# Fetching the chosen tokens' rows with indirect DMAs instead of one-hot products

## The chip, the core and the metric

The kernel runs on one core of a Trainium2 chip. The core has five engines, each with a queue of its own: TensorE for matrix products (PE; its weight loads are shown apart, as PEld), VectorE (DVE), ScalarE (ACT), GpSimd (POOL), and SyncE (SP), which here only issues transfers. The engines wait for each other through semaphores, and 16 DMA engines move data between the main memory (DRAM) and the on-chip memory (SBUF). Products land in a third memory, PSUM, from which VectorE or ScalarE must copy them ("evict" them).

The metric is the device time of one execution, in microseconds (us).

## The reference, cut to what matters

The program is a Fourier-layer network on 64 images of 256 x 256, whose output rows are joined with 77 text tokens and sent through one attention layer and one feed-forward layer that processes only a chosen part of the tokens. The change lies in that last layer:

```python
def _L0_ffn_ref(x, attention_mask, wr, br, w1, b1, w2, b2):
    weights = (jnp.einsum('bsd,do->bso', x, wr) + br)[..., 0]
    k = max(1, int(CAPACITY * s))
    kk = k - 1 if k > 1 else 1
    _, idx = jax.lax.top_k(weights, k)
    sel_idx = idx[:, :kk]
    sel = jnp.take_along_axis(x, sel_idx[:, :, None], axis=1)
    h = jax.nn.gelu(jnp.einsum('bkd,dh->bkh', sel, w1) + b1)
    y = jnp.einsum('bkh,hd->bkd', h, w2) + b2
    w_sel = jnp.take_along_axis(weights, sel_idx, axis=1)
    y = y * w_sel[..., None]
    processed = jnp.zeros_like(x).at[batch_idx, sel_idx].set(y)
    return processed + x
```

Each of the 64 samples has 333 tokens of 256 numbers. A router gives every token a weight, the 165 tokens of greatest weight go through the two products with a GELU between them, and their results are put back at the tokens' places, times the weight. All other tokens get zero there. Everything is float32.

## The kernel before

Most of the span is the Fourier network; it is the same in both kernels and plays no part here. The code of the change is the last stage, which works through the samples one by one. It is written for a framework that takes the instructions in the order of the program, looks at their dependencies, gives out buffers from pools, and then orders the instructions of each engine by a cost model of its own. So an engine's queue is not the order of the source: work of neighbouring samples is interleaved. Once built, the order is fixed, and each engine takes its instructions strictly in that order (on TensorE this holds for the products).

The main loop keeps three samples in flight. For sample b it runs:

- `image_rows(b + 2)`: loads the last layer's image in eight pieces `ch` of 1 MB on SyncE's queue (L894) and sums over channels with 32 products (L896, into `hp`); before it come small steps on `am` (L878, L882 on VectorE), the product L884, the eviction `y1`, and the products L889. ScalarE evicts `hp` to `h` (L901).
- `attention(b + 1)`: a layer norm (L910 to L918), transposes of it (L928), products for queries, scores and values (L974, L986, L1000), softmax, transposes of the probabilities (L1015, evicted to `probT`), the products with the values (L1024), then the residual: GpSimd adds a bias to `h` (L1020) and VectorE makes `h1` from it (L1027). A second layer norm gives `z` (the tile is called `fz`).
- `feed_forward(b)`: described below.
- `select(done[1])` for sample b + 1: the router. VectorE computes the weights (L940), three products with a matrix of ones (L945) spread them over all partitions, L947 adds the router's bias, and for each of the three tiles of tokens (128, 128 and 77) VectorE counts how many tokens have a greater weight (L954 to L963). That count is the token's rank, `gt`. L965 turns it into a row of a one-hot matrix: `place[token, rank]` is 1 where the token has that rank. `fw` is the weight where the rank is below 165 and zero elsewhere.

In `feed_forward` the one-hot matrix does the fetching and the putting back, with products on TensorE: `z` times `place` gives the 165 chosen rows, transposed, as `zs` (L1042); `place` is transposed to `back` (L1053); and after the two layers of the feed-forward (L1059, GELU, L1070) and a transpose of their result to `ys` (L1080), `back` times `ys` puts the results at their tokens (L1089), where VectorE multiplies by `fw` and adds `h1 + z` (L1092). GpSimd issues the 17 transfers of the output (L1097, L1101).

Evictions go through the helper `evict`, whose counter `flip` gives every second one of this stage to ScalarE and the others to VectorE. GpSimd's transfers use eight semaphores in turn, so one of them waits until the one eight before it has landed.

Of the kernel before, what the change touches and what calls it, by code (L numbers as in the profile page):

```python
# [8 lines left out]

F32 = mybir.dt.float32  # L10
AF = mybir.ActivationFunctionType
ALU = mybir.AluOpType
AX = mybir.AxisListType
# [3 lines left out]
S = 256  # L17
# [5 lines left out]
TOK = S + TXT  # L23
HID = 1024
EPS = 1e-5
KEPT = max(1, int(0.5 * TOK)) - 1
# [8 lines left out]
def _tables():  # L35

    y = np.arange(S)
    ky = np.arange(M)
    kx = np.concatenate([np.arange(M), np.arange(-M, 0)])
    th = 2 * np.pi * np.outer(y, ky) / S  # L40
    tx = 2 * np.pi * np.outer(y, kx) / S
    grid = np.linspace(0.0, 1.0, S, dtype=np.float32)
    p = np.arange(128)
    out = {}

    def halves(a):
        return a.reshape(2, 128, -1).transpose(1, 0, 2)

    def ravel(*dims):

        return np.unravel_index(np.arange(np.prod(dims)), dims)


    fy = np.zeros((S, 32))
    fy[:, :M], fy[:, M:KX] = np.cos(th), -np.sin(th)
    out["fyt"] = np.tile(fy.reshape(8, 32, 32).transpose(1, 0, 2), (4, 1, 1))
    ex = np.zeros((128, S))
    ex[:KX], ex[KX:2 * KX] = np.cos(tx).T, np.sin(tx).T
    ex[2 * KX], ex[2 * KX + 1] = 1, grid
    for n in range(4):  # L60
        ex[2 * KX + 2 + n, 64 * n:64 * n + 64] = 1
    ex[64:] = ex[:64]
    h, i, hq, r, j = ravel(2, 4, 4, 2, 4)
    hc = 4 * h + hq
    out["exE"] = ex[:, 64 * j + 16 * i + 2 * hc + r]
    out["exO"] = ex[:, 64 * i + 16 * j + 2 * hc + r]
    cs = np.concatenate([np.cos(tx), -np.sin(tx)], 1)
    sc = np.concatenate([np.sin(tx), np.cos(tx)], 1)
    csc = np.concatenate([cs, sc, cs], 1)
    j, b2, hh, g, r = ravel(4, 2, 2, 4, 2)  # L70
    for n in "EO":
        rows = []
        for h in range(2):
            a, b = (2 * h + b2, g) if n == "E" else (g, 2 * h + b2)
            rows.append(csc[64 * a + 16 * b + 2 * (2 * j + hh) + r])
        out["fx" + n] = np.stack(rows, 1)
    ck = np.where(ky == 0, 1.0, 2.0) / (S * S)
    t32 = np.zeros((32, S))
    t32[:M], t32[M:KX] = (np.cos(th) * ck).T, -(np.sin(th) * ck).T
    out["t4"] = np.tile(t32, (4, 1))  # L80
    out["ident"] = np.eye(128)
    out["ones"] = np.ones((128, 128))
    out["chan"] = p[:, None] % C == np.arange(C)[None, :]

    cr = np.zeros((2, 64, 4, 32))
    cr[:, 48, 0, 0] = cr[:, 48, 1, 28] = cr[:, 49, 2, 0] = 1
    for n in range(4):
        cr[:, 50 + n, 3, 24 + n] = 1
    out["crow"] = cr

    out["fyr"] = halves(fy)
    out["fyi"] = halves(np.concatenate([np.sin(th), np.cos(th), np.zeros((S, 8))], 1))
    out["fxn"] = halves(np.concatenate([cs, grid[:, None], np.zeros((S, 15))], 1))
    out["gyr"] = halves(np.repeat(grid[:, None], 128, 1))
    m6 = np.zeros((128, 3, 2, 4, C))
    for g in range(3):
        for r in range(2):
            for k4 in range(4):
                m6[M * r + 4 * g + k4 + 32 * np.arange(4), g, r, k4] = 1
    out["m6"] = m6  # L100
    out["mk4"] = p[:, None] % 4 == np.arange(128)[None, :] // C

    g = grid.astype(np.float64)
    one = np.ones(S)
    gh = np.zeros((128, 3, 2, KX))
    for j, (a, b) in enumerate(((g, one), (one, g), (one, one))):
        m = np.outer(np.exp(-1j * tx).T @ a, np.exp(-1j * th).T @ b)
        for k4 in range(4):
            gh[4 * j + k4] = np.stack([m.real, m.imag])[:, :, k4::4].transpose(2, 0, 1)
    out["gh"] = gh  # L110

    t, g, n, hc = ravel(2, 4, 4, 8)
    x_of = 64 * n + 16 * g + 2 * hc + t
    out["exT"] = ex[:, x_of]
    out["mask4"] = p[:, None] // C == np.arange(4)[None, :]
    tok = np.concatenate([x_of, S + np.arange(TXT)])
    rows = np.stack([x_of[:128], x_of[128:], S + p], 1)
    out["iota"] = np.repeat(np.arange(KEPT)[None, :], 128, 0)
    out["tri"] = tok[None, None, :] < rows[:, :, None]
    out = {k: np.ascontiguousarray(v.reshape(128, -1), np.float32) for k, v in out.items()}  # L120

    mv = np.zeros((4, 32, 16, S), np.float32)
    mv[:, :KX] = t32[None, :KX, None, :]
    mv[:, 28] = grid
    return out, mv.reshape(128, 16 * S)
# [10 lines left out]
def tile_fno_fusion_transformer(ctx: ExitStack, tc: tile.TileContext, a, cst_d, grid_d, out):  # L136
    nc = tc.nc
    x = a["x"].rearrange("b x y o -> b x (y o)")
    B = x.shape[0]
# [3 lines left out]
    small = ctx.enter_context(tc.tile_pool(name="small", bufs=4))  # L143
# [633 lines left out]
    s_, t_ = st  # L777
    tcon = ctx.enter_context(tc.tile_pool(name="tcon", bufs=1))
    inp = ctx.enter_context(tc.tile_pool(name="inp", bufs=7))
    tabt = tables(tcon, "exT", "tri", "cstt")  # L780
    EXT, MASK4, IOTA = tabt("exT"), tabt("mask4"), tabt("iota")
    TRI = tabt("tri").rearrange("p (t j) -> p t j", t=3)
    qrow = tcon.tile([128, C, 1], F32, name="qrow")
    nc.vector.tensor_mul(qrow[:, :, 0], qR, s_)
# [12 lines left out]
    D = S  # L797
# [70 lines left out]
    pb_ = ctx.enter_context(tc.tile_pool(name="tpb", bufs=2, space=PSUM))  # L868
    pp = ctx.enter_context(tc.tile_pool(name="tpp", bufs=6, space=PSUM))

    def psum():
        return pp.tile([128, 512], F32, name="pp")

    def image_rows(b):
        am = ap_.tile([2 * KX, 32 * C], F32, name="am")
# [53 lines left out]
            evict(zT[:, dh, :], ps[:, :TOK], 2)  # L929
        return z, zT  # L930

    def select(z):


        wcol = small.tile([128, 3], F32, name="wcol")
# [10 lines left out]
        wrow = tp.tile([128, TOK], F32, name="wrow")  # L946
        nc.vector.tensor_scalar(wrow, ps[:, :TOK], brB, None, ALU.add)  # L947
        fw = small.tile([128, 3], F32, name="fw")
        place = tp.tile([128, 3, KEPT], F32, name="place")
        for t in range(3):  # L950
            r = rows[t]
# [10 lines left out]
            )  # L962
            nc.vector.tensor_add(gt[:r], gt[:r], eq[:r])  # L963
            nc.vector.tensor_scalar(fw[:r, t:t + 1], gt[:r], float(KEPT), wc[:r], ALU.is_lt, ALU.mult)
            nc.vector.tensor_scalar(place[:r, t, :], IOTA[:r], gt[:r], None, ALU.is_equal)  # L965
        return fw, place

    def attention(h):
        z, zT = layer_norm(h, "a")
        qT = tp.tile([128, 2, TOK], F32, name="qT")  # L970
        for eh in range(2):
# [39 lines left out]
        for jt in range(3):  # L1011
# [2 lines left out]
            for t in range(3):  # L1014
                nc.tensor.transpose(ps[:r, toks[t]], p_[:rows[t], t, toks[jt]], ID[:rows[t], :rows[t]])  # L1015
            evict(pT[:r, jt, :], ps[:r, :TOK], 2)
        h1 = tp.tile([128, 3, D], F32, name="h1")
        for t in range(3):
            r = rows[t]
            nc.gpsimd.tensor_add(h[:r, t, :], h[:r, t, :], boB[:r])  # L1020
# [7 lines left out]
                h1[:r, t, :], ps[:r, :D], sm[:r, t:t + 1], h[:r, t, :], ALU.mult, ALU.add  # L1028
            )
        z = layer_norm(h1, "f")  # L1030
        return h1, z

    kept = [slice(0, (KEPT + 1) // 2), slice((KEPT + 1) // 2, KEPT)]

    def feed_forward(b, h1, z, fw, place):

        zs = tp.tile([128, 2, KEPT], F32, name="zs")
        for dh in range(2):
            ps = psum()
            for t in range(3):  # L1040
                r = rows[t]
                nc.tensor.matmul(  # L1042
                    ps[:, :KEPT], lhsT=z[:r, t, 128 * dh:128 * dh + 128], rhs=place[:r, t, :],
                    start=t == 0, stop=t == 2,
                )
            evict(zs[:, dh, :], ps[:, :KEPT], 2)
        back = tp.tile([128, 2, TOK], F32, name="back")
        for c, k in enumerate(kept):
            n = k.stop - k.start
            ps = psum()  # L1050
            for t in range(3):
                r = rows[t]
                nc.tensor.transpose(ps[:n, toks[t]], place[:r, t, k], ID[:r, :r])  # L1053
            evict(back[:n, c, :], ps[:n, :TOK], 2)
        g = tp.tile([128, HID // 128, KEPT], F32, name="g", bufs=1)
        for hb in range(HID // 128):
            ps = psum()
# [18 lines left out]
        for c, k in enumerate(kept):  # L1076
            n = k.stop - k.start
            ps = psum()
            for dh in range(2):
                nc.tensor.transpose(ps[:n, 128 * dh:128 * dh + 128], yT[:, dh, k], ID)  # L1080
            evict(ys[:n, c, :], ps[:n, :D], 2)
        o = tp.tile([128, 3, D], F32, name="o")
        for t in range(3):
            r = rows[t]
            nc.gpsimd.tensor_add(h1[:r, t, :], h1[:r, t, :], z[:r, t, :])
            ps = psum()
            for c, k in enumerate(kept):
                n = k.stop - k.start
                nc.tensor.matmul(  # L1089
                    ps[:r, :D], lhsT=back[:n, c, toks[t]], rhs=ys[:n, c, :], start=c == 0, stop=c == 1  # L1090
                )
            nc.vector.scalar_tensor_tensor(  # L1092
                o[:r, t, :], ps[:r, :D], fw[:r, t:t + 1], h1[:r, t, :], ALU.mult, ALU.add
            )
        for g in range(4):
            for n in range(4):
# [4 lines left out]
        nc.gpsimd.dma_start(out[b, S:TOK], o[0:TXT, 2, :])  # L1101

    hs = {n: image_rows(n) for n in range(min(2, B))}
    done = attention(hs.pop(0))
    done += select(done[1])
    for b in range(B):
        now = done
        if b + 2 < B:
            hs[b + 2] = image_rows(b + 2)
        if b + 1 < B:  # L1110
            done = attention(hs.pop(b + 1))
        feed_forward(b, *now)
        if b + 1 < B:
            done += select(done[1])


# [31 lines left out]
```

## Time and profile before

| what | value |
|---|---|
| time, median of 3 runs | 12373.28 us (12368.81 to 12376.6) |
| span of the profiled execution | 12358.8 us |
| TensorE busy | 11164.5 us, 90% |
| VectorE busy | 8774.8 us, 71% |
| ScalarE busy | 6094.5 us, 49% |
| GpSimd busy | 1412.7 us, 11% |
| mean data rate | 282 GB/s |

The spans differ a little from the times, as the profiled execution is one of its own. The page of a profile also cuts the span into 40 equal slices (of 309 us here) and gives each engine's busy share in tenths, and under PEclk the clock that TensorE was granted, in tenths of full speed. Shares of the whole span mix stages with different limits. In the timeline a row is a group of like instructions: start in us from the span's start, duration, engine, source line, operation, output and input tiles, the shape, the number of instructions, and in brackets how long the engine stood idle before it and which instruction's end let it go. One float32 product shows as two records, so the counts there are twice those of the program (a transpose shows as one).

### The profile page before, as it was taken

The numbers are of one execution on the slowest core, as the hardware profiler recorded it, in microseconds if no ns is written. First come the engines' busy times: TensorE is split into PE (matmuls) and PEld (weight loads), VectorE is DVE, ScalarE is ACT, GpSimd is POOL, SyncE is SP. The second block draws the span as 40 slices with busy tenths as digits, with TensorE's granted clock in tenths as the row PEclk, the third lists the DMA queues.
The fourth block names the chain that finished last, engine by engine and source line by source line (L and its number), as shares of the span: only waits on it lengthen the run. The fifth ranks groups of instructions, "written<-read, shape, count | busy, mean of one in ns | idle before, by whom it ended". The sixth has DMA issues, their size and how long they took to land. (4 is left out here: it accounts for less than half of the span.)

```text
span 12358.8 us, 405064 instructions
## 1 busy us (share of the span) xinstructions
PE 11164.5 (90%) x182038; PEld 5874.0 (48%) x182038; DVE 8774.8 (71%) x10667; ACT 6094.5 (49%) x10249; POOL 1412.7 (11%) x1987
## 2 busy tenths in 40 slices
PE   6999999998799999999979999999999699999999
PEld 3444444443444444444434444444444366666666
DVE  6777777777776777777766777767777566666665
ACT  5555555555555555555544555555555333333333
POOL 0000000000000000000010000000000133333333
PEclk8999999999899999999989999999999799999999
DMA  7555555555899999888889989889899755555554
GB/s 226 200 199 203 203 201 201 201 200 210 325 354 349 349 351 350 348 347 348 346 302 352 354 346 355 339 339 353 346 351 352 247 234 227 219 228 233 218 223 152
DMA packets 589283, 3485.06 MB, mean 282 GB/s; under 512 B 95000, under 2 KB 144536, under 8 KB 188568
## 3 DMA queue, kind: packets, MB, share of 16 engines
q1 hardware_dynamic: 539520, 3392.84, 71.2%
q0 software_dynamic: 40880, 62.59, 2.0%
q8 instruction: 1423, 23.31, 0.8%
q10 hardware_dynamic: 7144, 3.72, 0.1%
q14 instruction: 316, 2.59, 0.1%
HBM read 1761.87 MB, written 1696.92 MB: 280 GB/s over the span
## 5 line engine op out<-in xcount | busy, mean ns | idle before, releaser
L666 ACT ACTIVATE ring<-ring 128x1024 f32<-128x1024 f32 x3072 | 3108.8, 1012 | 1186.4 <-PE ring L659 1148.7
L647 DVE STREAM_TRANSPOSE t<-vo 128x2048 f32<-128x2048 f32 x1536 | 3550.0, 2311 | 175.1 <-ACT vo L642 14.5
L659 PE MATMUL ring<-vo,w 32*32 32x512 f32 x49152 | 2849.3, 622 | 392.2 <-DVE zt L686 138.7
L642 ACT ACTIVATE vo<-ring 128x1024 f32<-128x1024 f32 x1536 | 1568.2, 1021 | 2997.7 <-PE ring L635 2378.9
L643 DVE TENSOR_SCALAR vo<-ring 128x1024 f32<-128x1024 f32 x1536 | 1857.7, 1209 | 608.2 <-PE ring L635 420.4
L676 PE MATMUL ring<-t,cst 32*32 32x512 f32 x49152 | 1864.7, 601 | 303.7 <-issue 302.1
L686 DVE STREAM_TRANSPOSE zt<-ring 128x1024 f32<-128x1024 f32 x384 | 711.8, 1925 | 1658.6 <-PE ring L676 1658.6
L659 PEld LDWEIGHTS ring<-vo,w 32*32 32x32 f32 x49152 | 761.3, 105 | 1898.7 <-ACT ring L666 477.0
L676 PEld LDWEIGHTS ring<-t,cst 32*32 32x32 f32 x49152 | 975.9, 103 | 1157.0 <-issue 707.8
L594 POOL TENSOR_TENSOR ams<-am,sk 48x512 f32<-48x512 f32 x384 | 486.9, 1268 | 8642.4 <-DMA am<-mix 8039.9
L635 PE MATMUL ring<-vin,ws 32*32 32x512 f32 x32768 | 1238.0, 606 | 22.1 <-issue 19.8
L699 PEld LDWEIGHTS ring<-cst,zt 128*128 128x128 f32 x4608 | 536.4, 194 | 174.6 <-ACT vo L642 161.6
L666 ACT ACTIVATION_READ_ACCUMULATOR ring<-ring 128x1 f32 x3072 | 584.1, 190 | 0.0
L1097 POOL DMA_DIRECT2D out_dram<-o x1024 | 504.4, 501 | 659.8 <-DVE o L1092 628.2
L699 PE MATMUL ring<-cst,zt 128*128 128x96 f32 x4608 | 568.7, 281 | 8.1 <-DVE zt L686 8.1
L896 PE MATMUL hp<-ch,win 128*32 128x512 f32 x4096 | 472.0, 601 | 8.3 <-DMA ch<-v 8.1
L635 PEld LDWEIGHTS ring<-vin,ws 32*32 32x32 f32 x32768 | 253.5, 103 | 407.9 <-issue 377.8
L605 PE MATMUL ring<-ams,cst 49*128 49x512 f32 (+1 forms) x1536 | 391.5, 621 | 37.6 <-POOL ams L594 27.2
L901 ACT ACTIVATE h<-hp,hbias 128x512 f32<-128x512 f32 x64 | 44.0, 687 | 595.5 <-PE hp L896 595.5
L419 PE MATMUL mps<-wm,xh 32*64 32x128 f32 (+1 forms) x4608 | 121.3, 374 | 203.4 <-ACT e L431 74.1
L1059 PE MATMUL pp<-zs,w 128*128 128x165 f32 x2048 | 302.1, 305 | 0.0
L1070 PE MATMUL pp<-g,w 128*128 128x165 f32 x2048 | 298.6, 303 | 0.0
(936 smaller groups left out, 11812.8 us busy)
## 6 DMA issues: line engine op xcount, KB each, us to landing
v<-vo SPq DMA_DIRECT2D x1536, 1024.0 KB
vin<-v SPq DMA_DIRECT2D x1024, 1024.0 KB
ch<-v SPq DMA_DIRECT2D x512, 1024.0 KB
mix<-ob SPq DMA_DIRECT2D x96, 512.0 KB
am<-mix SPq DMA_DIRECT2D x384, 96.0 KB
xin<-in_x_dram SPq DMA_DIRECT2D x16, 1024.0 KB
mv<-in_x_dram SPq DMA_DIRECT2D x256, 64.0 KB
out_dram<-o POOLq DMA_DIRECT2D x1024, 16.0 KB, 3.0
```

Source lines behind the costliest of these rows:

```text
L594: nc.gpsimd.tensor_tensor(ams[b % 2][hv], a_[hv], sk[hv].rearrange("p c k -> p (c k)"), ALU.mult)
L635: nc.tensor.matmul(ps[n][32 * j:32 * j + 32], lhsT=ws[32 * n:32 * n + 32], rhs=v[32 * n:32 * n + 32, 2 * j:2 * j + 2, :], start=False, sto ...
L642: nc.scalar.activation(of[:, 0:2], t2[0], AF.Relu)
L643: nc.vector.tensor_scalar(of[:, 2:4], t2[1], 0.0, None, ALU.max)
L647: nc.vector.transpose(t32[b, t // 2][:, :, 8 * (t % 2):8 * (t % 2) + 8, :].rearrange("p y s c -> p s y c"), o.rearrange("p s (y l) -> p s ...
L659: nc.tensor.matmul(ps[n][32 * j:32 * j + 32], lhsT=w4[i + 1][32 * n:32 * n + 32], rhs=o[32 * n:32 * n + 32, 2 * j:2 * j + 2, :], start=Tru ...
L666: nc.scalar.activation(t2[n], t2[n], AF.Square, accum_out=acc[:, at:at + 1])
L676: nc.tensor.matmul(ps[n][32 * j:32 * j + 32], lhsT=FYT[32 * n:32 * n + 32, k, :], rhs=t32[b, j][32 * n:32 * n + 32, k].rearrange("p s c -> ...
L686: nc.vector.transpose(zt[:, h].rearrange("p k c -> p c k"), t2[h].rearrange("p n (s c) -> p c (n s)", c=C),)
L699: nc.tensor.matmul(ps[:, 0, 96 * g:96 * g + 96], lhsT=zt[:, h, k0:k0 + 4, :].rearrange("p k c -> p (k c)"), rhs=FX[:, h, 48 * r:48 * r + 9 ...
L896: nc.tensor.matmul(hp[32 * g:32 * g + 32], lhsT=win[:, 7 - t:39 - t], rhs=ch[:, g], start=False, stop=t == 7, skip_group_check=True,)
L1097: nc.gpsimd.dma_start(out[b, 64 * n + 16 * g:64 * n + 16 * g + 16].rearrange("(p t) d -> p t d", t=2), o[32 * g + 8 * n:32 * g + 8 * n + 8 ...
```

## The change

The one-hot products that move rows are taken away, and rows are moved by DMA instead, with indices that the kernel computes.

- After the second layer norm, `attention` stores `z` to a DRAM buffer `z_d`, three GpSimd transfers a sample (L1064 of the new file).
- `select` still makes `place`, but uses it only in small products (L991): `place` times a table `tokn` of token numbers, two equal columns wide, gives for each rank the number of the token that has it. VectorE turns it into whole numbers, `who` (L994), and GpSimd issues two indirect transfers (L995) that fetch those rows of `z_d` into `zr`. A further VectorE instruction keeps the rank, at most 165, as a whole number, `idx` (L981).
- `feed_forward` transposes `zr` to get `zs` (four transposes L1074, one eviction). After `ys` is there, two transfers store it to a DRAM buffer `y_d` (L1106), and three indirect ones (L1110) fetch for each token the row of its rank into `o`. Row 165 of `y_d` is zero, written once at the start, for all tokens that were not chosen.
- The last step, times `fw` plus `h1 + z` and the output transfers, becomes a function `finish` (L1119, L1124), which the loop calls one sample later. `h1` gets a third buffer, and `z_d` and `y_d` are three buffers each.

The new lines are shifted against the old ones: L1059, L1070 and L1080 are L1082, L1093 and L1103 in the new file, L896 is L911, L945 is L960, L882 is L897, L878 is L893, L974, L986, L1000, L1015 and L1024 are L1006, L1018, L1032, L1047 and L1056, and L1020 is L1052.

```diff
@@ select
         fw = small.tile([128, 3], F32, name="fw")
+        idx = small.tile([128, 3], U32, name="idx")
...
+            nc.vector.tensor_scalar(idx[:r, t:t + 1], gt[:r], float(KEPT), None, ALU.min)
             nc.vector.tensor_scalar(place[:r, t, :], IOTA[:r], gt[:r], None, ALU.is_equal)
-        return fw, place
+        ps = psum()
+        who = small.tile([128, 2], U32, name="who")
+        zr = tp.tile([128, 2, D], F32, name="zr")
+        for c, k in enumerate(kept):
+            n = k.stop - k.start
+            for t in range(3):
+                r = rows[t]
+                nc.tensor.matmul(
+                    ps[:n, 2 * c:2 * c + 2], lhsT=place[:r, t, k], rhs=TOKN[:r, t, :], start=t == 0, stop=t == 2
+                )
+            nc.vector.tensor_copy(who[:n, c:c + 1], ps[:n, 2 * c:2 * c + 1])
+            nc.gpsimd.indirect_dma_start(
+                zr[:n, c, :], None, z_d[b % 3][:, :], bass.IndirectOffsetOnAxis(ap=who[:n, c:c + 1], axis=0)
+            )
+        return fw, idx, zr
@@ attention
-        h1 = tp.tile([128, 3, D], F32, name="h1")
+        h1 = tp.tile([128, 3, D], F32, name="h1", bufs=3)
...
         z = layer_norm(h1, "f")
+        for t in range(3):
+            nc.gpsimd.dma_start(z_d[b % 3][128 * t:128 * t + rows[t]], z[:rows[t], t, :])
@@ feed_forward
-        for dh in range(2):
-            ps = psum()
-            for t in range(3):
-                r = rows[t]
-                nc.tensor.matmul(
-                    ps[:, :KEPT], lhsT=z[:r, t, 128 * dh:128 * dh + 128], rhs=place[:r, t, :],
-                    start=t == 0, stop=t == 2,
-                )
-            evict(zs[:, dh, :], ps[:, :KEPT], 2)
-        back = tp.tile([128, 2, TOK], F32, name="back")
+        ps = psum()
         for c, k in enumerate(kept):
             n = k.stop - k.start
-            ps = psum()
-            for t in range(3):
-                r = rows[t]
-                nc.tensor.transpose(ps[:n, toks[t]], place[:r, t, k], ID[:r, :r])
-            evict(back[:n, c, :], ps[:n, :TOK], 2)
+            for dh in range(2):
+                nc.tensor.transpose(
+                    ps[:, KEPT * dh + k.start:KEPT * dh + k.stop], zr[:n, c, 128 * dh:128 * dh + 128], ID[:n, :n]
+                )
+        evict(zs.rearrange("p h k -> p (h k)"), ps[:, :2 * KEPT], 2)
...
+        for c, k in enumerate(kept):
+            nc.gpsimd.dma_start(y_d[b % 3][k], ys[:k.stop - k.start, c, :])
         o = tp.tile([128, 3, D], F32, name="o")
         for t in range(3):
             r = rows[t]
+            nc.gpsimd.indirect_dma_start(
+                o[:r, t, :], None, y_d[b % 3][:, :], bass.IndirectOffsetOnAxis(ap=idx[:r, t:t + 1], axis=0)
+            )
             nc.gpsimd.tensor_add(h1[:r, t, :], h1[:r, t, :], z[:r, t, :])
-            ps = psum()
-            for c, k in enumerate(kept):
-                n = k.stop - k.start
-                nc.tensor.matmul(
-                    ps[:r, :D], lhsT=back[:n, c, toks[t]], rhs=ys[:n, c, :], start=c == 0, stop=c == 1
-                )
+        return o, h1, fw
+
+    def finish(b, o, h1, fw):
+        for t in range(3):
+            r = rows[t]
             nc.vector.scalar_tensor_tensor(
-                o[:r, t, :], ps[:r, :D], fw[:r, t:t + 1], h1[:r, t, :], ALU.mult, ALU.add
+                o[:r, t, :], o[:r, t, :], fw[:r, t:t + 1], h1[:r, t, :], ALU.mult, ALU.add
             )
@@ the loop
         if b + 1 < B:
-            done = attention(hs.pop(b + 1))
-        feed_forward(b, *now)
+            done = attention(b + 1, hs.pop(b + 1))
+        if last:
+            finish(b - 1, *last)
+        last = feed_forward(b, *now)
         if b + 1 < B:
-            done += select(done[1])
+            done += select(b + 1, done[1])
+    finish(B - 1, *last)
```

More of the change, by code (lines that the diff above doesn't have):

```diff
@@ L10 @@
 F32 = mybir.dt.float32
+U32 = mybir.dt.uint32
 AF = mybir.ActivationFunctionType
@@ L118, in _tables @@
     out["iota"] = np.repeat(np.arange(KEPT)[None, :], 128, 0)
+    t_ = np.stack([np.arange(128), 128 + np.arange(128), S + p], 1).astype(np.float64)
+    out["tokn"] = np.repeat(t_, 2, 1)
     out["tri"] = tok[None, None, :] < rows[:, :, None]
@@ L781, in tile_fno_fusion_transformer @@
     EXT, MASK4, IOTA = tabt("exT"), tabt("mask4"), tabt("iota")
+    TOKN = tabt("tokn").rearrange("p (t n) -> p t n", t=3)
     TRI = tabt("tri").rearrange("p (t j) -> p t j", t=3)
@@ L869, in tile_fno_fusion_transformer @@
     pp = ctx.enter_context(tc.tile_pool(name="tpp", bufs=6, space=PSUM))
+    kept = [slice(0, (KEPT + 1) // 2), slice((KEPT + 1) // 2, KEPT)]
     def psum():
         return pp.tile([128, 512], F32, name="pp")
+    z_d = [dram.tile([TOK, D], F32, name=f"zr{n}") for n in range(3)]
+    y_d = [dram.tile([KEPT + 1, D], F32, name=f"yr{n}") for n in range(3)]
+    zero = tcon.tile([1, D], F32, name="zero")
+    nc.vector.memset(zero, 0.0)
+    for q in y_d:
+        nc.gpsimd.dma_start(q[KEPT:KEPT + 1], zero)
     def image_rows(b):
@@ L930, in layer_norm, with select @@
         return z, zT
-    def select(z):
+    def select(b, z):
         wcol = small.tile([128, 3], F32, name="wcol")
@@ L964, in select, with attention @@
             nc.vector.tensor_scalar(fw[:r, t:t + 1], gt[:r], float(KEPT), wc[:r], ALU.is_lt, ALU.mult)
+            nc.vector.tensor_scalar(idx[:r, t:t + 1], gt[:r], float(KEPT), None, ALU.min)
             nc.vector.tensor_scalar(place[:r, t, :], IOTA[:r], gt[:r], None, ALU.is_equal)
-        return fw, place
-    def attention(h):
+        ps = psum()
[13 more added lines that the diff above has]
+        return fw, idx, zr
+    def attention(b, h):
         z, zT = layer_norm(h, "a")
@@ L1030, in attention, with feed_forward @@
         z = layer_norm(h1, "f")
+        for t in range(3):
+            nc.gpsimd.dma_start(z_d[b % 3][128 * t:128 * t + rows[t]], z[:rows[t], t, :])
         return h1, z
-    kept = [slice(0, (KEPT + 1) // 2), slice((KEPT + 1) // 2, KEPT)]
-    def feed_forward(b, h1, z, fw, place):
+    def feed_forward(b, h1, z, fw, idx, zr):
         zs = tp.tile([128, 2, KEPT], F32, name="zs")
-        for dh in range(2):
-            ps = psum()
-            for t in range(3):
-                r = rows[t]
-                nc.tensor.matmul(
-                    ps[:, :KEPT], lhsT=z[:r, t, 128 * dh:128 * dh + 128], rhs=place[:r, t, :],
-                    start=t == 0, stop=t == 2,
-                )
-            evict(zs[:, dh, :], ps[:, :KEPT], 2)
-        back = tp.tile([128, 2, TOK], F32, name="back")
+        ps = psum()
         for c, k in enumerate(kept):
             n = k.stop - k.start
-            ps = psum()
-            for t in range(3):
-                r = rows[t]
-                nc.tensor.transpose(ps[:n, toks[t]], place[:r, t, k], ID[:r, :r])
-            evict(back[:n, c, :], ps[:n, :TOK], 2)
+            for dh in range(2):
[3 more added lines that the diff above has]
+        evict(zs.rearrange("p h k -> p (h k)"), ps[:, :2 * KEPT], 2)
         g = tp.tile([128, HID // 128, KEPT], F32, name="g", bufs=1)
@@ L1103, in tile_fno_fusion_transformer @@
     hs = {n: image_rows(n) for n in range(min(2, B))}
-    done = attention(hs.pop(0))
-    done += select(done[1])
+    done = attention(0, hs.pop(0))
+    done += select(0, done[1])
+    last = None
     for b in range(B):
@@ L1110, in tile_fno_fusion_transformer @@
         if b + 1 < B:
-            done = attention(hs.pop(b + 1))
-        feed_forward(b, *now)
+            done = attention(b + 1, hs.pop(b + 1))
+        if last:
+            finish(b - 1, *last)
+        last = feed_forward(b, *now)
         if b + 1 < B:
-            done += select(done[1])
+            done += select(b + 1, done[1])
+    finish(B - 1, *last)
 _INS = [
```

## The prediction

> **What bounds the kernel now.** I read the page's 40 slices first, to place the changed code in the span; then the busy time of a stretch of that stage; then TensorE's timeline inside one sample; last the few spots where TensorE did wait.
>
> ```profile
> PE   6999999998799999999979999999999699999999
> POOL 0000000000000000000010000000000133333333
> PEclk8999999999899999999989999999999799999999
> 10000.00:12000.00 2000.00, 1953.01 (x11930) 1360.61 (x11931) 1353.21 (x4850) 758.64 (x1548) 654.99 (x1150) 1.00 0.58 226
> ```
>
> The fusion layer is where GpSimd shows 3: the last eight slices, some 2,550 us for 64 samples. The fourth line is a stretch of it: the columns after the length are PE, PEld, DVE, ACT and POOL busy, then granted clock, DMA share and GB/s. TensorE is busy 97.7% of it at clock 1.00; VectorE 68%, ScalarE 38%, GpSimd 33%, DMA 58%. L1059 comes back every 40.0 us (9949.93, 9989.92, 10029.90 in the chain that ended last), so one sample costs 40.0 us and TensorE sets it.
>
> ```profile
> 10707.63 1.85 PE L1042 MATMUL pp<-place,fz 128*128 128x165 f32 x12
> 10709.32 0.74 PE L1053 MATMUL pp<-cst,place 128*83 128x128 f32 x6
> 10709.90 4.70 PE L1059 MATMUL pp<-zs,w 128*128 128x165 f32 x32
> 10719.58 0.45 PE L1080 MATMUL pp<-cst,yT 128*83 128x128 f32 x2 [0.27 <-ACT yT L1074]
> 10720.44 2.87 PE L1089 MATMUL pp<-ys,back 83*128 83x256 f32 x12 [0.40 <-DVE ys L178]
> 10723.14 0.61 PE L945 MATMUL pp<-dg,cst 128*128 128x128 f32 x4
> ```
>
> From start to start: gather products L1042 1.69 us, transposes of `place` L1053 0.58, scatter products L1089 2.70, and 0.40 of waiting for `ys` ahead of them. All four are on the engine that sets the end.
>
> ```profile
> 12317.97 0.45 PE L945 MATMUL pp<-dg,cst 77*128 77x77 f32 x2 [0.36 <-DVE dg L944]
> 12321.46 0.80 PE L1042 MATMUL pp<-place,fz 128*128 128x165 f32 x4 [3.04 <-DVE place L965]
> 9852.88 1.39 PE L974 MATMUL pp<-azT,wqk 128*128 128x333 f32 x4 [1.80 <-DVE azT L178]
> 9854.40:9857.60 3.20, 3.20 (x6) 2.04 (x7) 1.66 (x5) 1.91 (x3) 1.77 (x3) 0.51 1.02 430
> 12322.40:12328.40 6.00, 5.40 (x21) 4.97 (x20) 3.03 (x14) 0.73 (x2) 3.26 (x7) 0.50 0.15 33
> ```
>
> These are the spots that decide my forecast. Once, for the last sample, TensorE has nothing to put between the router's last product (L945) and the first product that reads `place`: it idles 3.04 us, since VectorE must first rank a tile. After that idle the clock is 0.50 for 6 us; after the single idle of 1.80 us at 9851 it is 0.51 for 3.2 us.
>
> **What the Trainium skill says.** (1) "TensorE: Matmul & The Clock Gate", Part 2, step 1: weight loads are pulled ahead, but "The MATMULs themselves stay in program order". So a product that waits holds back everything behind it; 12321.46 agrees. (2) The same page, Part 1: the clock goes to half after an idle window of about 3.4 us. The trace differs: 1.80 us of idle were enough. I use the trace. (3) "DMA: Bandwidth & Descriptors", Anatomy of one DMA: about 2.0 us fixed per GpSimd DMA, most of it the receipt of the write. The trace agrees on idle queues (1.8 us to landing for the first output DMAs of a sample, 1.9 for 77 rows at the end) but has 6 to 7 us once the `ch` loads fill the engines. (4) The same page, Two DMAs through the same engine are not ordered: the reader must wait for the writer's semaphore; here it does.
>
> **The change, part by part.** Besides the diff I use the order in which the built program holds each engine's instructions. It gives two alternating patterns, X and Y, because a sample now has 9 shared evictions instead of 12, so the VectorE/ScalarE turn flips each sample.
>
> *Removed from TensorE:* 1.69 + 0.58 + 2.70 + 0.40 = 5.37 us a sample; and two of the L960 products now stand in the 0.27 us gap before the second pair of L1103. Together 5.6 us.
>
> *Added to TensorE:* six products of 2 columns (L991), near 0.12 each with their weight loads (nine transposes L1015 take 1.03 us): 0.7. Four transposes L1074: 0.45. Then L1082 must wait for one eviction of 330 columns (probT's 333 take 0.49) with nothing left to cover it: 0.6. In sum 1.75. With no other wait a sample would take 40.0 - 5.6 + 1.75 = 36.1 us.
>
> *The new wait for `place`.* The first L991 stands directly behind the last L960, ahead of the image products of the sample after the next. Let T be the end of the last L1103 and count from there. `ys` is evicted until 0.35; L962 starts at 0.4; from it to the end of the first `place` it took 2.85 us at the end of the span (12318.46 to 12321.31), plus 0.13 for the new `idx` instruction: 3.4. TensorE is ready at 0.3: 3.1 us idle, each sample. Before, this VectorE work lay under L928, L889 and L896.
>
> *The other waits, tile by tile.* Of rank work a tile costs VectorE about 1.8 us. In X: `y1` (0.4) in between, second `place` at 5.75, third only behind `azT` (0.5) and two of the three L1119 that `finish` puts there (0.48 each): 9.05. TensorE gets there at 8.0, after one wait of 0.25 for `y1`. Second half of L991: its PSUM tile is shared, so it waits for the first `who` copy, which stands behind the third L1119 and L897 (1.9): 11.5 against 11.0. Waits: 0.25 + 1.05 + 0.5 = 1.8. In Y: L897 stands ahead of the second tile (7.25 against 5.7), the third comes at 10.3 against 10.05, and L893 (1.2) is covered: 1.55 + 0.25 = 1.8.
>
> *Later in the sample:* all three score tiles end close together in the new order (L1018 by halves), so VectorE's reductions and the `probT` copies come bunched: I count 0.7 of waiting before and in L1056. Sum: 36.1 + 3.1 + 1.8 + 0.7 = 41.7 us.
>
> *The clock.* 3.1 us idle in a sample is more than the 1.80 that halved the clock for 3.2 us. Such a stretch defers 1.6 us of products; part falls into waits that are there anyway. I take 0.6 and keep 0 and 2.5 as ends. So 42.3.
>
> *The DMAs.* Each sample adds 333 + 165 + 165 + 333 rows of 1 KB, 1.0 MB, to 9 MB: 2.5 us of DMA time at the 400 GB/s of the busy stretch, where the engines stand idle 16 of 40 us. Not a bound. GpSimd gets ten more issues. Stores cost 0.50 to 0.53 each; an indirect one is in no row: at least 0.53, as 77 rows cost, at most some 2.5; I take 1.2. GpSimd then has 13.2 + 5 x 0.5 + 5 x 1.2 = 21.7 of 42. It also holds eight DMAs in flight (each waits for the one eight before), so outputs at 6.5 us landing go at 0.8 apiece; the add L1052 behind them starts near 26, and its result is wanted at 27.
>
> *The return path.* `ys` at 0.4, stores landed at 3.0 (1.9 after issue; the engines are idle there), gathers issued at 3.1, 4.3, 5.5, landed near 6.0, 7.2, 9. VectorE reaches the three L1119 at 7.4, 8.0 and 9.0 in X, later in Y: hidden, just. The `zr` gathers go out at 12 and 13.5 and are read at 30: hidden even at 8 us. At 2.5 an issue the third result lands near 12 and adds 2 to 3 us, since L1119 stands ahead of the last `place` and the `who` copies. L1049's third buffer and the third `z_d` and `y_d` only keep slots from binding: nothing.
>
> *The ends.* The last sample's stores, gathers and `finish` come one after another: +6.5 us against 2.9 for its L1089: +4. Sum: 12373 + 62 x 2.3 + 4 = 12520 us.
>
> **The rivals.** *A, faster:* the waits overlap better than I count, say half of the 5.6 us of them is gone, and no clock loss: 38.9 us, 12373 - 68 = 12305; with none but the 3.1 it would be 39.2. For it: 5.6 us surely leave the bound engine. Against: the 3.04 us wait is measured, and stands in every sample's queue. *B, a wash:* waits equal savings, 40.0 us, 12375. *C, much slower:* indirect issues near 2.5 us, DMA landing late, or TensorE at half clock over two windows as at 12322: 46 us, 12373 + 372 = 12745. For it: the 6 us stretch at 0.50; against: the queues are idle when `ys` goes out.
>
> **How the numbers follow.** My case (41 to 44.5 us) 0.62, C 0.17, A 0.14, B 0.07. Predicted 12520. The range 12400 to 12700 (40.4 to 45.2 us) holds my case with both ends of the clock and most of the indirect cost; A, B and the worst of C are left out. Faster 0.14, same 0.07, slower 0.79.
>
> **What would show it.** In the changed profile: no rows for the removed lines; TensorE below 90% in this stage; L991 waiting some 3 us for DVE `place` in each sample; PEclk below 1.00 in it; period about 42 us. Wrong, if L991 waits under 1 us, if L1119 waits long for the gather (then C), or if L1074 waits for `zr`.

## The result and the profile after

The changed kernel takes 12775.62 us (median of 4 runs, 12773.36 to 12794.07), the one before 12371.59 us in the same comparison: ratio 1.0329, 95% interval 1.0311 to 1.0347. It is slower by 404 us, or 6.5 us in each of 62 samples; I had forecast 147.

The page's slices, and the busy times of a stretch of the fusion layer (PE, PEld, DVE, ACT, POOL, then granted clock, DMA share, GB/s):

```profile
PE   6999999997999999999789999999996888888887
POOL 0000000001000000000100000000002444544445
PEclk8999999998999999999989999999997889888898
...
10100.00:12100.00 2000.00, 1764.49 (x9553) 1160.78 (x9551) 1264.86 (x4278) 617.96 (x1253) 982.02 (x1408) 0.88 0.60 213
```

L1074 comes 43 times in this stretch, so a sample takes 2000 / 43 = 46.5 us, against 40.0. TensorE is busy 1764 / 43 = 41.0 us of it and idle 5.5. It has less to do than before, and is busy longer: its mean clock is 0.88. GpSimd works 22.8 us a sample.

What TensorE waited for in the same stretch (total us, times, longest), some rows of its timeline, and two short stretches in the columns of the one above (L179 and L181 are `evict`):

```profile
PE pp L991 <- DVE place L982: 130.0, 43, 3.0
PE pp L1074 <- DMA zr<-zr,who: 56.7, 43, 3.3
PE pp L1082 <- DVE zs L181: 13.1, 22, 0.6
PE pp L1056 <- DVE probT L181: 11.3, 16, 0.7
PE pp L1082 <- ACT zs L179: 11.0, 21, 0.5
...
11016.40 0.31 PE L991 MATMUL pp<-cstt,place 128*83 128x2 f32 x2 [3.02 <-DVE place L982]
11019.92 5.33 PE L911 MATMUL hp<-ch,win 128*32 128x512 f32 x18
11025.42 1.92 PE L911 MATMUL hp<-ch,win 128*32 128x512 f32 x16
11048.80 0.36 PE L1074 MATMUL pp<-cst,zr 82*128 82x82 f32 x2 [3.30 <-DMA zr<-zr,who]
11049.75 7.74 PE L1082 MATMUL pp<-zs,w 128*128 128x165 f32 x32 [0.59 <-DVE zs L181]
...
11018.31:11024.90 6.59, 6.59 (x24) 1.78 (x22) 5.04 (x14) 0.00 (x0) 3.60 (x6) 0.50 0.49 155
11049.40:11055.80 6.40, 6.05 (x22) 6.05 (x23) 5.95 (x12) 3.21 (x7) 6.08 (x12) 0.50 0.15 39
```

Two waits lead: 3.0 us for `place` and 1.3 for `zr`. Behind each the products run slowly: 18 records of L911 take 5.33 us where 16 take 1.92 a little later, and L1082 takes 7.74 us where L1059 took 4.70 before. In both places the clock is 0.50. A mean of 0.88 means half clock in 24% of the time, some 11 us of a sample.

The chain that ended last, in this part (start, us, what), shows the fetch:

```profile
11016.13 0.23 DVE place L982
...
11025.52 0.16 DVE who L994
...
11027.49 0.23 POOL zr L995
...
11030.38 18.37 DMA zr<-zr,who
```

From issue to landing (the arrival of all its data) the fetch of 82 or 83 rows takes 15 to 18 us in this chain. GpSimd, whose transfers share eight semaphores, waits for it as well: 534 us in this stretch at L1124. So one sample hands on to the next through a closed loop: feed-forward, ranking, `who`, issue, landing, transposes of `zr`, feed-forward.

### The profile page after: what moved, and what is told of

The parts are those of the page before. It is cut to its first block, busy times and chain, and to the rows that moved or that the text cites. A ratio compares the mean times of both kernels' runs of the same rounds, so it can differ in the third digit from the quotient of the medians.

```text
span 12771.5 us, 404517 instructions
## 1 busy us (share of the span) xinstructions
PE 11291.5 (88%) x181142; PEld 5846.3 (46%) x181142; DVE 8934.2 (70%) x10892; ACT 6056.8 (47%) x10153; POOL 2048.5 (16%) x2630
## 5 line engine op out<-in xcount | busy, mean ns | idle before, releaser
L911 PE MATMUL hp<-ch,win 128*32 128x512 f32 x4096 | 685.5, 713 | 1.1 <-DMA ch<-v 1.1
L1124 POOL DMA_DIRECT2D out_dram<-o x1024 | 537.4, 531 | 914.9 <-DMA zr<-zr,who 741.3
L1082 PE MATMUL pp<-zs,w 128*128 128x165 f32 x2048 | 370.1, 348 | 36.7 <-DVE zs L181 19.9
L1082 PEld LDWEIGHTS pp<-zs,w 128*128 128x128 f32 x2048 | 354.1, 224 | 47.1 <-DVE zs L181 25.1
L1056 PE MATMUL pp<-v,probT 128*128 128x256 f32 (+3 forms) x1152 | 269.5, 387 | 33.2 <-DVE probT L181 16.3
```

Of the source, the lines that this page charges most:

```text
L911: nc.tensor.matmul(hp[32 * g:32 * g + 32], lhsT=win[:, 7 - t:39 - t], rhs=ch[:, g], start=False, stop=t == 7, skip_group_check=True,)
L1082: nc.tensor.matmul(ps[:, :KEPT], lhsT=w1[:, dh, 128 * hb:128 * hb + 128], rhs=zs[:, dh, :], start=dh == 0, stop=dh == 1,)
L1124: nc.gpsimd.dma_start(out[b, 64 * n + 16 * g:64 * n + 16 * g + 16].rearrange("(p t) d -> p t d", t=2), o[32 * g + 8 * n:32 * g + 8 * n + 8 ...
```

## The experiments

Differences of some 10 us between the medians of the kernel before (12360 to 12372) are the noise of these comparisons.

**The two halves alone.** x1 keeps the fetch of the rows and puts the results back with `back` and L1089 of before, and its last step is not put off; x2 keeps the one-hot L1042 of before and puts the results back through DRAM.

In x1:

```diff
...
-            nc.gpsimd.indirect_dma_start(
-                o[:r, t, :], None, y_d[b % 3][:, :], bass.IndirectOffsetOnAxis(ap=idx[:r, t:t + 1], axis=0)
-            )
...
+                nc.tensor.matmul(
+                    ps[:r, :D], lhsT=back[:n, c, toks[t]], rhs=ys[:n, c, :], start=c == 0, stop=c == 1
+                )
...
```

In x2:

```diff
...
-                nc.tensor.transpose(
-                    ps[:, KEPT * dh + k.start:KEPT * dh + k.stop], zr[:n, c, 128 * dh:128 * dh + 128], ID[:n, :n]
-                )
...
+                nc.tensor.matmul(
+                    ps[:, :KEPT], lhsT=z[:r, t, 128 * dh:128 * dh + 128], rhs=place[:r, t, :],
+                    start=t == 0, stop=t == 2,
+                )
...
```

> Half of the change: the rows of z are fetched by token number as in the changed kernel, the results go back by the one-hot products of before (back, one buffer). Theory A (the fetch of zr carries the loss: its rows land 15 to 18 us after the issue, and the wait for place takes TensorE's clock): the time stays near the changed kernel's, 12650 to 12900 us, with a wait of 1 us or more at the transposes of zr. Rival (the way back through DRAM, its GpSimd queue and the held output DMAs carry it): 12450 us or less.

> The other half: tokens are gathered by the one-hot products of before, the results come back by rank through DRAM as in the changed kernel. Theory A (the fetch of zr carries the loss): this half only takes the products of the way back (2.70 us) and the transposes of place (0.58 us) off TensorE, and is faster than before: 12130 to 12280 us. Rival (the way back carries the loss): 12500 us or more.

Measured: x1 13091.7 us (ratio 1.0585, 1.0567 to 1.0603), x2 12691.68 us (1.0273, 1.0255 to 1.0291). Each half alone is slower than before, which neither theory had: x1 lies above the numbers of both, x2 at the rival's. The traces say why (each run has line numbers of its own). A wait of x1, then its chain:

```profile
POOL zr L988 <- DVE who L987: 245.5, 39, 8.1
...
11025.32 0.59 PE pp L1077 x6
...
11037.03 2.01 PE pp L1113 x8
...
11048.12 0.55 POOL out_dram L1125
11048.67 5.99 issue
...
11057.28 19.22 DMA zr<-zr,who
```

The loop through `zr` is still there, and the transposes to `back` (L1077) and the products of the way back (L1113) now stand inside it, between the landing and the ranking: 3.7 us by the times of before (0.58, 2.70 and the 0.40 of waiting). A sample of x1 is 5.1 us longer than one of the changed kernel; the rest is open. The 17 output issues of a sample also stand ahead of the fetch in GpSimd's queue, but they do not hold it: GpSimd is through with them and then waits 245.5 us in 39 samples, 6.3 each, for `who` (what the chain calls "issue" here). x2:

```profile
11032.73 1.98 DMA yr<-ys
...
11040.78 7.80 DMA o<-yr,idx
...
11048.68 0.48 DVE o L1102
...
11049.56 0.66 DVE abs L924 x2
...
11051.63 3.70 PE pp L1002 x6
```

Here the loop goes through VectorE's queue. The last step (L1102) waits for the fetched results, and the layer norm of a later sample (L924), which doesn't need them, stands behind it. TensorE waits for its outcome: 225.7 us over 43 samples at L1002, up to 7.0 each.

**96 rows in a fetch.** x3 and x5 fetch 96 rows each in place of 83 and 82; the extra index entries are zero. x3 clears a fresh `who` in each sample, x5 uses four fixed tiles cleared once.

```diff
...
+            nc.vector.memset(who, 0)
...
-                zr[:n, c, :], None, z_d[b % 3][:, :], bass.IndirectOffsetOnAxis(ap=who[:n, c:c + 1], axis=0)
+                zr[:96, c, :], None, z_d[b % 3][:, :], bass.IndirectOffsetOnAxis(ap=who[:96, c:c + 1], axis=0)
```

> The changed kernel with who cleared to 0 first and the two fetches of zr taking 96 rows each in place of 83 and 82 (the 27 extra rows are row 0 and are read by nobody). Theory E (83 and 82 rows are cut over one or two DMA engines, 96 over sixteen): the fetch lands 4 to 8 us after its issue in place of 15 to 18, the 3.3 us wait at the transposes of zr and the 10 us hold of the output DMAs go, and the time is 12500 to 12650 us. Rival S (the queue is starved under the ch loads, whatever the rows): landing stays at 15 to 18 us and the time at 12750 to 12800 us.

> As the run with 96 rows, but who lives in four fixed tiles that are cleared once at the start, so that no clearing stands in VectorE's queue behind an earlier fetch. Theory L (a closed loop of latencies from one sample to the next sets the period: products of the feed-forward, ranking, who, issue on GpSimd, 15 to 18 us of landing, transposes of zr): the fetch lands in 7 to 8 us, no wait is left at the transposes of zr, and what remains is the 3.0 us wait for place with its clock loss: 12560 to 12680 us. Rival R (the way back through VectorE's queue holds the period too): 12730 us or more.

Measured: x3 12762.82 us (1.0326, 1.0305 to 1.0347), x5 12747.22 us (1.0314, 1.0296 to 1.0331). The transfer did what E said, the time did not. The median landing in the lists of DMA issues, first of x1 with 83 and 82 rows, then of x3; GpSimd's software queue on the pages of the changed kernel and of x3 (packets, MB, share; a packet is what a DMA engine moves at a time); and the packets of all queues on the same two pages:

```profile
zr<-zr,who POOLq DMA_INDIRECT x16, 17.7
...
zr<-zr,who POOLq DMA_INDIRECT x18, 7.0
...
q0 software_dynamic: 100368, 128.39, 3.8%
...
q0 software_dynamic: 71696, 129.70, 3.6%
...
DMA packets 648775, 3550.84 MB, mean 278 GB/s; under 512 B 136633, under 2 KB 187321, under 8 KB 248057
...
DMA packets 620103, 3552.15 MB, mean 278 GB/s; under 512 B 106616, under 2 KB 157176, under 8 KB 219384
```

Two fetches of 96 rows move more bytes in 28672 / 64 = 448 fewer packets a sample, and land in 7.0 us. The issue on GpSimd falls from 1.76 to 0.98 us. The Trainium skill, "DMA: Bandwidth & Descriptors", "Why a DMA increments its semaphore by 16 and not by 1", has the likely reason: a transfer runs on the largest number of engines, up to 16, that divides its row count (some direct copies issued by GpSimd are excepted), which gives 1 for 83, 2 for 82 and 16 for 96. The engines of a single transfer are in no view here, but the packet counts fit exactly. Taking four rows to a packet, 83 rows on one engine make 21 packets, 82 on two make 22, and two fetches of 96 on sixteen make 64, so x3 should have 21 more. It has 30017 fewer under 512 bytes, 469 a sample, and 469 is 15 x 21 + 14 x 11: as many small packets for each engine without rows as an engine with rows has. 469 less 21 is the 448. What the small packets do is not shown.

The wait for `zr` on TensorE is gone in both, yet little time is. In x3 the clearing of `who` waits on VectorE for an earlier fetch (124.8 us over 21 samples): a fault of the experiment, which x5 mends. In x5 the next limits show: the 3.0 us for `place`, 64.4 us of waits for `o` on VectorE, and 61.9 us for `probT` on TensorE. E's and L's numbers were missed, rival R's came true.

One thing more stands in x5's chain on the way to `probT`. A VectorE multiplication of 128 x 1 (L1044), 0.16 us in the median, takes 2.10 us from 11044.49 on, just as GpSimd's three additions L1055 take 2.09 us from 11044.48 on. x2 has the same once a sample in the part of its chain that I read (L1025, 2.46 and 2.47 us).

**Filling the wait for `place`.** x4 puts four products whose result nobody reads between L960 and L991.

```diff
...
+        for _ in range(4):
+            nc.tensor.matmul(ps[:, 64:64 + TOK], lhsT=ONES, rhs=wrow, start=True, stop=True)
...
```

> The changed kernel with four extra products of ONES and wrow (128 x 333, results unused, some 3 us in all) put on TensorE between the row products and the first products on place, so that the 3.0 us of idle there are filled. Theory C (that idle stretch makes the clock fall to half for 3 us or more, and this sets the period): granted clock 0.98 or more, the products that took 7.74 us take 4.7 us again, and the time is 12540 to 12650 us. Rival W (the late landing of zr sets the period by itself): the wait at the transposes of zr grows by what the products save, 12720 to 12790 us.

Measured: 12697.32 us (1.0268, 1.025 to 1.0285). The clock in the stretch rises from 0.88 to 0.97, and 78 us are gained: between the two theories. TensorE waits for the ranking as long as before, only elsewhere: 29.4 us for `wrow`, 35.6 for `place` and 66.4 for `who` in the stretch, against 130.0 for `place`. GpSimd still waits 516 us for the late `zr` at the outputs.

**Splitting the feed-forward.** x6 (96 rows) and x7 (83 and 82) put the router between its two halves (`up` and `down`), and the fetch of `who` and `zr` after them.

```diff
...
-        last = feed_forward(b, *now)
-        if b + 1 < B:
-            done += select(b + 1, done[1])
...
+        g = up(b, zr)
+        if b + 1 < B:
+            done += select(b + 1, done[1])
+        last = down(b, g, h1, z, fw, idx)
+        if b + 1 < B:
+            done += (fetch(b + 1, done[-1]),)
```

> The changed kernel with 96 rows as before and the source reordered: the feed-forward is cut in two, the router's products and the ranking of the next sample stand between the halves, and the products on place with the fetch follow the second half. Theory L: TensorE no longer waits for place (the second half, 4.5 us, stands over the ranking) and the fetch goes out some 3 us after the feed-forward, so nothing of the loop is left longer than TensorE's own 36 to 38 us of work: 12130 to 12280 us, clock 0.98 or more. Rival R (the way back or GpSimd's queue holds 43 us or more by itself): 12500 us or more.

> The same reordered kernel with the fetches of 83 and 82 rows of the changed kernel. Theory L: 15 to 18 us of landing fit between the issue, some 5 us after the feed-forward, and the next one, some 26 us after it, so it costs 100 us at most against the run with 96 rows: 12150 to 12350 us. Rival D (the long landing costs by itself, as it holds the eight semaphores of GpSimd's transfers and all issues behind it): 12500 us or more.

Measured: x6 12951.48 us (1.0478, 1.0461 to 1.0496), x7 13269.41 us (1.0731, 1.0708 to 1.0755). Theory L falls in this form. The wait for `place` did vanish (14.7 us in 2000), but in x6 VectorE waits 399.9 us for `o` and TensorE 267.3 us for `azT`, which stands behind it. x7 takes 318 us more than x6, where L allowed 100.

**The last step two samples later.** x8 is x2 with `finish` called two samples later in the source (`finish(b - 2, ...)`, one more buffer for `h1` and `o`, two more for `fw`, one fewer for `zs`).

> The half with the results fetched back through DRAM, with the last step of a sample called two samples later in place of one (h1 and o with one buffer more, zs with one less). Theory L: in the first run of this half the period was the loop o fetched, last step, layer norm behind it in VectorE's queue, attention, feed-forward, ys stored, o fetched; with a sample more that loop has 70 us or more of room, the 7.0 us wait at the scores goes, and the time is 12130 to 12280 us. Rival G (GpSimd's queue of 22 issues and the stores and fetches in it holds the period): 12550 us or more.

Measured: 12559.11 us (1.0155, 1.0135 to 1.0176): 133 us better than x2, but far from L's number and at rival G's. The same wait is there (272.8 us for `o` in 2000). The built programs explain it: VectorE, ScalarE and TensorE have the same instructions in the same order in x2 and x8, and only GpSimd's order and the buffers differ. In both, the cost model has the last step directly behind that sample's own fetches, with only ranking work of the next sample between, although x8's source calls it two samples on. Here a call's place in the source did not hold an instruction back. This gave theory M: readers stand where a short landing would allow them, and a late landing stalls the whole queue behind them.

**The last step tied.** In x9 to x12 and x14, `fw` passes through an instruction that adds zero times `rs` of the second layer norm of the sample after the next.

```diff
...
+            fl = small.tile([128, 1], F32, name="fl")
+            nc.vector.scalar_tensor_tensor(
+                fl[:r], ties[-1][:r, t:t + 1], 0.0, fw[:r, t:t + 1], ALU.mult, ALU.add
+            )
...
-                o[:r, t, :], o[:r, t, :], fw[:r, t:t + 1], h1[:r, t, :], ALU.mult, ALU.add
+                o[:r, t, :], o[:r, t, :], fl[:r], h1[:r, t, :], ALU.mult, ALU.add
...
```

x9 is x2 so tied, x10 is x5, x11 is x6, x12 is x7, x14 is the changed kernel.

> The half with the results fetched back, with its last step made to depend on the second layer norm of the next sample but one (fw passes through a small instruction that adds zero times its rs). So the last step stands in VectorE's queue behind fz, some 25 us after the fetches, in place of directly behind where the built order takes them to have landed. Theory M (the built order puts the readers of each fetch where a short landing would allow it; the fetch lands 4 to 9 us late, and everything behind the reader in VectorE's queue, the layer norm first, waits as well, in each sample): the wait of VectorE for o (6 us a sample) and the 7.0 us wait at the scores vanish, period 36 to 38 us, 12130 to 12280 us. Rival G (GpSimd's queue holds the period whatever VectorE does): 12450 us or more.

> The whole change with 96 rows in each fetch (fixed who tiles) and the tied last step. Theory M: no wait for DMA is left on VectorE or TensorE; what is left is the 3.0 us wait for place with its clock loss, so the time falls from 12747 to between 12520 and 12680 us. Rival G: 12720 us or more.

> The split feed-forward with 96 rows and the tied last step. Theory M: the 12.5 us wait at the queries (for azT, behind the last step in VectorE's queue) and the wait for place are both gone, clock 0.97 or more, period 36 to 39 us: 12130 to 12330 us. Rival G (GpSimd's queue, 22 us of issues with their waits, holds it): 12600 us or more.

> The same with fetches of 83 and 82 rows. Theory M: the fetch goes out some 10 us after the feed-forward and lands 15 to 18 us later, about when its transposes come up at 25 us: 0 to 200 us more than with 96 rows, 12150 to 12500 us. Rival D (the late landing holds all of GpSimd's transfers behind it): more than 250 us over the run with 96 rows.

| run | us | ratio to before, 95% interval |
|---|---|---|
| x9 return only, tied | 12091.65 | 0.9787 (0.9771 to 0.9803) |
| x10 96 rows, tied | 12626.96 | 1.0214 (1.0197 to 1.0231) |
| x11 split, 96 rows, tied | 12312.82 | 0.9961 (0.9947 to 0.9975) |
| x12 split, 83 and 82 rows, tied | 12398.58 | 1.0027 (1.0016 to 1.0038) |

M's numbers hold in x10, x11 and x12, and x9 is better than they said. G is out: GpSimd is busy 968 us of the stretch in x9, against 842 in x8, and the sample is shorter. Three instructions a sample (0.14 to 0.70 us each in x9) took 600 us off x2 and 639 off x6. x9 beats both kernels: 2.1% (2.0 to 2.3) under the one before. The same stretch of x9, and what is left of waits in it:

```profile
10100.00:12100.00 2000.00, 1917.29 (x12071) 1375.56 (x12069) 1487.95 (x5583) 794.58 (x1651) 968.43 (x1578) 0.99 0.71 253
...
PE pp L1042 <- ACT probT L179: 21.2, 54, 0.4
```

TensorE is busy 96% at clock 0.99. A sample takes 4.4 us less than before, (12364.23 - 12091.65) / 62, so 35.6; 3.7 of the 4.4 are the work and the wait of the way back. x9 keeps the one-hot fetch, so its first product on `place` (L1059, 11036.54) starts 23.8 us after the router's last (L961, 11012.79), and TensorE's idle of 3.0 us does not arise. x12 against x11 prices the late landing in this form: 86 us.

**The clock by itself.** x13 is x10 with the filler of x4; x14 is the changed kernel with the tie alone.

> The run with 96 rows and the tied last step, and the four products of ONES and wrow ahead of the products on place, which fill the wait for place with work of no use. The sample stays as long there; only the clock can gain. Theory C (the 3 us of idle make the products after it run at half clock, some 3.3 us a sample: TensorE was busy 40.0 us a sample in the run with 96 rows and the tie, 36.7 in the split one): clock 0.98 or more, 12370 to 12480 us. Rival W (the wait itself is all that place costs): 12580 us or more.

> The changed kernel with nothing but the tied last step (fetches of 83 and 82 rows). Theory M: VectorE waited only 0.9 us a sample for o here, since the late landing of zr held everything anyway, so the tie moves little: 12690 to 12790 us. Rival O (the place of the last step in VectorE's queue holds the changed kernel as it held its second half): 12620 us or less.

Measured: x13 12434.03 us (1.006, 1.0044 to 1.0077), x14 12874.04 us (1.0414, 1.0392 to 1.0436). The same stretch of x10, x13 and x11:

```profile
10100.00:12100.00 2000.00, 1800.79 (x10140) 1169.51 (x10139) 1228.88 (x4665) 639.70 (x1328) 939.11 (x1485) 0.90 0.64 228
```

```profile
10100.00:12100.00 2000.00, 1885.60 (x11278) 1273.56 (x11276) 1323.96 (x5010) 685.85 (x1431) 1010.63 (x1601) 1.00 0.68 244
```

```profile
10100.00:12100.00 2000.00, 1873.47 (x11554) 1260.45 (x11553) 1370.56 (x5297) 718.96 (x1505) 1065.39 (x1691) 1.00 0.73 259
```

Work of no use makes the kernel 193 us faster, 3.1 us a sample: theory C. By samples in the stretch (45, 49, 51) TensorE is busy 40.0, 38.5 and 36.7 us a sample; 2.5 of the 38.5 are filler. So the idle for `place`, 3.2 us in x10 (143.4 in 45 samples), costs about as much again as itself, in products at half clock. x11, where the second half of the feed-forward stands over the ranking, saves both and takes 314 us off x10.

In x14 the tie alone made things worse by 98 us, against both theories' numbers. Its trace has TensorE waiting longer for `zr` (76.8 us in place of 56.7) and GpSimd 468.5 us for `who` ahead of the fetch (84.8 in the changed kernel). So the late reader of `o` did not hold the changed kernel by itself. The late landing does hold x14: x10 differs only in its fetches of 96 rows (and fixed `who` tiles) and is 247 us faster. The fetches of `o` stand behind those of `zr` in both and are late with them, 17.1 us in the median in x14 and 7.9 in x10. Why exactly the new order lengthens that loop I did not test further.

## Why the prediction was wrong

The direction was right, and the changed kernel lies nearest to rival C (46 us a sample, 12745), for two of the three reasons that C gave: late landing and half clock. The wait of L1074 for `zr`, named as a sign of being wrong, is there.

- *Removed and added on TensorE:* right. Without waits I had 35.5 us of work a sample (36.1 with the wait for `zs`); x13 has 36.0 besides its filler, x11 36.7.
- *The wait for `place`, 3.1:* right, 3.02 in each sample. *`zs` 0.6:* right, (13.1 + 11.0) / 43 = 0.56. *`probT` 0.7:* 0.45.
- *The other waits, 1.8:* not in the timeline; with slow products TensorE comes late to the second and third `place`. In x4, at clock 0.97, they are there: 35.6 + 66.4 us in 44 samples, 2.3 each.
- *The clock, "I take 0.6":* the failed term. TensorE's work of 36.0 to 36.7 us took 41.0, so 4.3 to 5.0; the part that hangs on `place` alone measures 3.1 in x13. Even the upper end of 2.5 was too small. I had taken the 3.2 us of half clock that followed the 1.80 us idle; the stretch shown behind `place` has it for 6.6 us, and a second stretch follows. I had also assumed that half-clock time would fall into waits. It fell on the image products and the feed-forward, which have none.
- *"The `zr` gathers go out at 12 and 13.5 and are read at 30: hidden even at 8 us":* wrong. They went out at 14 and 17 and landed 15 to 18 us after their issue. I took the landing from the output transfers in the trace of before, which have other shapes. The wait is only 1.3 us a sample, but it closes the loop, and a second idle stretch, ahead of L1082, brings a second spell of half clock.
- *The return path, "hidden, just":* true in the changed kernel (0.9 us a sample at L1119). In x2, without the loop through `zr`, it was the bound.
- *Indirect issue, 1.2:* 1.5 to 2.0 us for 83 and 82 rows, 0.97 to 1.38 for the returns. *DMA rate not a bound:* right, 213 GB/s.

In a sum: 35.5 of work, 6.2 of waits and 0.6 for the clock gave 42.3; it was 41.0 busy, clock loss included, and 5.5 idle. The causes do not add up one by one. Filling the `place` wait alone gave 78 us, 96 rows alone 28; 96 rows with the tie 149, and with the filler on top 342; the tie alone cost 98.

## What to carry to other kernels

Where a one-hot product is replaced by a trip through DRAM, look for the closed loop from one sample to the next and add up every landing in it; then ask what stands in the queue behind each reader, for it waits too. If a cost model orders the instructions, calling the reader later in the source may do nothing, while a cheap false dependency held it back. It was worth 600 us in x9, and cost 98 in x14, where another loop held. The idle of 3 us on TensorE cost about twice its length here, so look for other work to put there. Choose row counts for a fetch with care: 96 rows landed in less than half the time of 83.

## What the runs showed of the hardware

- A fetch of 82 or 83 rows of 1 KB lands in 15 to 18 us beside loads, one of 96 rows in 7.0, with 448 fewer packets for the two; the issue falls from 1.76 to 0.98 us. Fetches of 128 and 77 rows issued behind it land late too: 17.1 us in x14, 7.9 in x10.
- An idle of 3.2 us on TensorE cost another 3.1 us a sample in products at half clock (x10 against x13), so that useless products in its place made the kernel 1.5% faster.
- A VectorE instruction of 0.16 us took 2.10 us, as long as the GpSimd additions that ran beside it (x5, L1044 and L1055).
